# A three-stage kernel for one NeuronCore: three of the run-up rounds of its recurrence made before the last attention block is finished

## The chip, the cores and the metric

The kernel runs on one core of a Trainium2 chip, in one launch. The metric is the device time of that launch in microseconds (us). All data is float32.

## The reference, cut to what matters

The input x has 4 batches of 128 channels and 64 by 64 = 4096 tokens. Three layers follow each other:

- Layer 0 is attention over all tokens with 64 channels per head row, and its output is added to x.
- Layer 1 is causal attention with 128 channels over the normalised tokens, and its output is added too.
- The last layer normalises the tokens, multiplies them by W, normalises each of the 128 channels over all batches and tokens (a batch norm: mean and variance of 4 x 4096 values), and runs a recurrence along the tokens. Its result is added to the tokens:

```
Wx = (flat - mean) * rsqrt(var + eps) * gamma + beta
y[t] = sigmoid(Wx[t] + y[t-1] @ V.T)        # y[-1] = 0, 4096 tokens, 4 batches
```

The 4096 steps of the recurrence depend on each other. V is orthogonal and the slope of the sigmoid is at most 0.25, so a wrong start is forgotten within some rounds.

## The kernel before, in words

`fast_path` does the work. A second path, `general_path`, follows in the program and is entered only if a flag says that a result is out of range.

**Attention.** The tokens of a batch are 8 blocks of 512. A long list of items (a block of queries against a pair of key tiles) is worked off in one loop: `scores` puts a product into the PSUM tile `s_ps` (two buffers of two banks each, pool `ps_s`) and an exponential on ACT (L937), `values` two items later multiplies the exponentials `p` into `acc` (L990), and `sums` adds them up on DVE (L961, L969). What a finished block still needs hangs on chains of steps with due times (`finish0`, `finish1`), which the loop takes up between items.

**The last block** (batch 3, block 7) has a short form of its own in `finish1`, marked `final`. PE sums the softmax denominators (`den_ps`, L615); ACT and DVE each copy half of `acc` into `agg` (L1010, L1011); four products with `wv1` (`o_ps`, L643) are added to the tokens on DVE (L667); DVE takes moments (L676, L677), POOL raises to the power -0.5 (L681), and DVE and ACT each scale two of four tiles into `xh` (L695, L693). PE transposes them (`xh2T_ps`, L821), DVE and ACT each copy half (L822), PE multiplies by W (`wx_ps`, L851), DVE takes statistics of it (`ends`, L852) and ACT copies it into the tensor `xs` (L853). PE has two groups of idle work there, `warm_ps` (L790): 9 products after `o_ps` and 6 after `wx_ps`, whose results nobody reads. `spare` (L796) is a sigmoid of one column, which loads the sigmoid's table into ACT.

**Statistics.** Each block's `wx_ps` gives statistics into `stats`. When 31 of the 32 blocks are done, `ahead` (L730 to L732) folds them into three numbers of `ends`; the last block adds two more groups, and after it `mv` (L1171) and eight small instructions (L1175 to L1183) make `scale`, `shift` and `shift_half`, the batch norm as one multiplication and one addition.

**The recurrence.** The 4096 tokens of a batch are cut into 256 chunks of 16 steps, and all chunks of a batch run side by side as 256 columns. One round is one step of all chunks of the four batches: for each batch a product with V on PE (`y_ps`, L1222), a multiplication and addition on DVE (`z`, L1224) and a sigmoid on ACT (L1228). A chunk's start is not known, so ten run-up rounds (`WARM = 10`, steps -10 to -1) go over the last ten steps of the chunk before. The first of them starts from an assumed state of 0.5 and needs no product: it is one sigmoid per batch on ACT (L1219). Round -1 writes `start`. Rounds 0 to 15 give the result.

From round 4 on, each round has a `residual` after batch 1: four transposes on PE and one addition on DVE to `xr` (L1260), which is then sent out (L1261). POOL makes the sums of batches 0 and 1 from `xc` (`add`, L1235), sent out by L1237; the tile `sum` has three buffers. Both `xc` (8 loads of 512 KB, L1158) and `xr` (4 loads of 1 MB, L1168) are copies of the tokens that wait in DRAM, in `x2c` and `x2t`; all loads and outputs are issued by SP, in order. At the end `meet` (L1244 to L1248) squares the gap between each chunk's end and the start that the next chunk assumed, sums the squares per channel, and `judge` sets the flag.

**What orders the work.** Each engine has one queue and works it off in order. The order is made by a scheduler, except where `keep_in_program_order` pins an instruction. Waits between engines are counts on semaphores. A pool that is opened where older pools lay in memory makes its tiles wait for the last users of that memory: `xc`, `xr`, `mv` and `start` lie where the pools of the attention lay.

Of the kernel before, what the change touches and what calls it, by code (L numbers as in the profile page):

```python
# [9 lines left out]
F32 = mybir.dt.float32  # L10
# [350 lines left out]
def fast_path(  # L361
# [31 lines left out]
    WARM, TOL = 10, 2e-6  # L393
# [17 lines left out]

    def load(engine, name, shape, *parts):
        t = const.tile(shape, F32, name=name)
        for dst, src in parts:
            engine.dma_start(out=dst(t), in_=src)
        return t
# [22 lines left out]
    fold = const.tile([P, P], F32, name="fold")  # L439
# [22 lines left out]
    g1 = const.tile([P, P], F32, name="g1")  # L462
# [8 lines left out]
    spare = const.tile([P, 1], F32, name="spare")  # L471
# [10 lines left out]
    with tc.tile_pool(name="batch", bufs=1) as batch, tc.tile_pool(name="rows", bufs=2) as rowp, tc.tile_pool(  # L482
# [120 lines left out]
        def folded(den, by_pe):  # L603


            sq = wk.tile([P, TPB, Q, S], F32, tag="sq", name="sq")
            nc.vector.transpose(out=sq.rearrange("p j q s -> p (j q s)"), in_=den)
            part = stat.tile([P, Q, TPB], F32, tag="part", name="part")
            nc.vector.tensor_reduce(part, sq.rearrange("p j q s -> p q j s"), AX.X, ALU.add)
            own = stat.tile([P, Q, TPB], F32, tag="own", name="own")  # L610
            if by_pe:


                dp = misc("den_ps")[:, : TPB * Q]
                nc.tensor.matmul(dp, lhsT=fold, rhs=part.rearrange("p q j -> p (q j)"), start=True, stop=True)  # L615
                ins = nc.vector.tensor_tensor(own, dp.rearrange("p (q j) -> p q j", q=Q), quarter, ALU.mult)
                if copied:

                    tc.add_manual_dep(
                        ins.ins,  # L620
                        copied[0].ins.name,
                        mybir.DependencyInfo(mybir.DependencyClass.NoSync, mybir.DependencyReason.DATA),
                        reason="order on DVE",
                    )
            else:

                by_token = dram2.tile([Q, S, Q, TPB], F32, tag="by_token", name="by_token")
                for k in range(Q):
                    nc.sync.dma_start(out=by_token[:, :, k].rearrange("q r j -> r q j"), in_=part[ts(k, S)])
                nc.sync.dma_start(out=own, in_=by_token.rearrange("q r k j -> (q r) k j"))  # L630
            return own
# [7 lines left out]
        def projected1(agg):  # L639

            op = misc("o_ps")
            for j in range(TPB):
                nc.tensor.matmul(op[:, ts(j, P)], lhsT=agg[:, ts(j, P)], rhs=wv1, start=True, stop=True)  # L643
            return op
# [41 lines left out]
        def normed(b, g, dst, mv, half, y, last=False):  # L686

            newton(y, half, stat.tile([P, TPB], F32, tag="z", name="ln_z"), not last)
            for j in range(TPB):
                if last:  # L690
                    t = xs[:, b, ds(g * BLK + j * P, P)]
                    if j % 2:
                        nc.scalar.activation(dst[:, j], t, AF.Copy, scale=y[:, j : j + 1])  # L693
                    else:
                        nc.vector.tensor_scalar(dst[:, j], t, y[:, j : j + 1], None, ALU.mult)  # L695
                    continue
                nc.vector.tensor_scalar(  # L697
                    dst[:, j], xs[:, b, ds(g * BLK + j * P, P)], mv[:, j, 0:1], y[:, j : j + 1], ALU.subtract, ALU.mult
                )
# [27 lines left out]
        def ahead():  # L727

            mv = stat.tile([P, nc.vector.BN_AGGR_DIM], F32, tag="mv1", name="mv1")
            nc.vector.bn_aggr(mv, stats)  # L730
            nc.vector.tensor_copy(ends[:, 1:2], mv[:, 0:1])
            nc.vector.tensor_tensor(ends[:, 2:3], mv[:, 1:2], ends[:, 0:1], ALU.mult)  # L732

# [46 lines left out]
        def finish1(b, g, turn):  # L780
# [4 lines left out]
            def warm(n, rhs):  # L785

                ps = ps_s.tile([P, 2 * BLK], F32, tag="s", name="warm_ps")
                for _ in range(n):
                    tc.keep_in_program_order(
                        nc.tensor.matmul(ps[:, : BLK // 2], lhsT=ident, rhs=rhs, start=True, stop=True)  # L790
                    )

            def first():
                if final:

                    nc.scalar.activation(spare, agg[:, 0:1], AF.Sigmoid)  # L796
                denominators(1, b, g, mem["own"])
                joined(1, b, g, mem["op"] if turn else projected1(agg))
                if final:
                    warm(9, agg[:, : BLK // 2])  # L800
# [13 lines left out]
            def second():  # L814
                mem["xhT"] = wk.tile([P, BLK], F32, tag="xhT2", name="xhT2")
                if final:
                    for k, copy in enumerate((nc.vector.tensor_copy, nc.scalar.copy)):
                        ps = misc("xh2T_ps")
                        for i in range(2):

                            nc.tensor.transpose(ps[:, ts(i, P)], mem["xh"][:, 2 * k + i], ident)  # L821
                        copy(mem["xhT"][:, ts(k, BLK // 2)], ps[:, : BLK // 2])  # L822
                    return
# [21 lines left out]
            def third():  # L845

                to = xs[:, b, ts(g, BLK)].rearrange("p (s c) -> p s c", s=STEPS)
                if final:
                    for k in range(2):
                        wp = misc("wx_ps")[:, : BLK // 2]  # L850
                        nc.tensor.matmul(wp, lhsT=wfc, rhs=mem["xhT"][:, ts(k, BLK // 2)], start=True, stop=True)  # L851
                        nc.vector.bn_stats(ends[:, 3 + 6 * k : 9 + 6 * k], wp)  # L852
                        nc.scalar.copy(to[:, :, ts(k, CPB // 2)], wp.rearrange("p (c s) -> p s c", s=STEPS))  # L853
                    warm(6, mem["xhT"][:, : BLK // 2])
                    return
# [13 lines left out]
            def sums():  # L869
                mem["own"] = folded(den, by_pe)  # L870
# [41 lines left out]
        def scores(it):  # L912
# [16 lines left out]
            else:  # L929
# [7 lines left out]
                nc.scalar.activation(it.p[:, :off], ps[:, :off], AF.Exp, scale=float(P) ** -0.5)  # L937
# [33 lines left out]
        def values(it):  # L971
# [16 lines left out]
            else:  # L988
                for h, (t, q0, n, o) in enumerate(it.at):
                    nc.tensor.matmul(  # L990
# [5 lines left out]
                    )  # L996
            if it.last:
# [9 lines left out]
                else:  # L1007
                    bt.agg = wk.tile([P, BLK], F32, tag="agg", name="agg")
                    if it.b == B - 1 and it.g == NB - 1:
                        nc.scalar.copy(bt.agg[:, : BLK // 2], bt.acc[:, 0, : BLK // 2])  # L1010
# [64 lines left out]
        def begin(s):  # L1075
            nonlocal done
            if done < s < len(items):
                done = s
                it = items[s]
                if it.first:  # L1080
# [4 lines left out]
                scores(it)  # L1085

# [62 lines left out]
    with tc.tile_pool(name="xr", bufs=1) as xrp, tc.tile_pool(name="y", bufs=2) as yp, tc.tile_pool(  # L1149
# [22 lines left out]
        one = lambda name: xrp.tile([P, 1], F32, name=name)  # L1172
        var, y, half, nmean, z = one("var"), one("y0"), one("var_half"), one("nmean"), one("z0")
        scale, shift, shift_half = one("scale"), one("shift"), one("shift_half")
        nc.vector.tensor_scalar(var, mv[:, 1:2], BN_EPS, None, ALU.add)  # L1175
        nc.gpsimd.tensor_tensor(y, var, mhalf[:, :1], ALU.pow)
        nc.vector.tensor_scalar(half, var, -0.5, None, ALU.mult)
        nc.vector.tensor_scalar(nmean, mv[:, 0:1], -1.0, None, ALU.mult)
        nc.vector.scalar_tensor_tensor(z, in0=y, scalar=half, in1=y, op0=ALU.mult, op1=ALU.mult)
        nc.vector.scalar_tensor_tensor(y, in0=z, scalar=1.5, in1=y, op0=ALU.add, op1=ALU.mult)  # L1180
        nc.vector.tensor_tensor(scale, y, gamma, ALU.mult)
        nc.vector.scalar_tensor_tensor(shift_half, in0=nmean, scalar=scale, in1=beta_half, op0=ALU.mult, op1=ALU.add)
        nc.vector.scalar_tensor_tensor(shift, in0=nmean, scalar=scale, in1=beta, op0=ALU.mult, op1=ALU.add)  # L1183

        by_step = xs.rearrange("p b (g s c) -> p b s g c", s=STEPS, c=CPB)
        start = xrp.tile([P, B, NCH + 1], F32, name="start")
        nc.gpsimd.memset(start[:, :, 0:1], 0.0)
        prev = [None] * B
        grid = lambda t: t.rearrange("p (g c) -> p g c", c=CPB)
# [14 lines left out]
        pin = tc.keep_in_program_order  # L1204

        def step(b, s):
# [11 lines left out]
            if prev[b] is None:  # L1218
                nc.scalar.activation(grid(y), wx, AF.Sigmoid, scale=scale, bias=shift_half)  # L1219
            else:  # L1220
                ps = ps_y.tile([P, NCH], F32, tag=f"y{b}", name="y_ps")
                order(nc.tensor.matmul(ps if s < 1 else shaped(ps), lhsT=vf, rhs=prev[b], start=True, stop=True))  # L1222
                z = yp.tile([P, NCH], F32, tag=f"z{b}", name="z")
                ins = nc.vector.scalar_tensor_tensor(  # L1224
                    grid(z), in0=wx, scalar=scale, in1=grid(ps), op0=ALU.mult, op1=ALU.add
                )
                order(ins)
                order(nc.scalar.activation(y, shaped(z), AF.Sigmoid, bias=shift))  # L1228
# [13 lines left out]
        def meet(b):  # L1242
# [5 lines left out]
            nc.scalar.activation(sq, ps, AF.Square, accum_out=gap[:, b : b + 1])  # L1248
# [37 lines left out]
        def judge():  # L1286
            total = xrp.tile([P, 1], F32, name="total")
            tc.keep_in_program_order(nc.vector.tensor_scalar(count[:, :B], gap, TOL * TOL, None, ALU.is_le))
# [70 lines left out]
```

## Time and profile before

| What | us |
|---|---|
| median of 3 runs (2024.64 to 2025.42) | 2025.14 |
| the profiled execution's own time | 2024.73 |
| its span in the profile | 2023.0 |
| last exponential of the attention starts | 1946.7 |
| first sigmoid of the recurrence starts | 1961.6 |
| round -1 starts on ACT | 1978.15 |
| the flag is written | 2019.56 |

The profile is one execution, taken by the hardware profiler; its times are counted from the start of the span, and 1.7 us of the execution lie around it. PE is busy for 99% of the span, DVE for 72%, ACT for 48% and POOL for 7%. A row "start, us, engine, line, operation, out<-in, xN" is one group of instructions; brackets at its end give the engine's idle time before it and what ended that. PEld is the weight load of a product. A float32 product is two passes on PE, so a line's count of records is twice its products.

### The profile page before, as it was taken

How to read it: one execution, taken by the hardware profiler on the slowest of the kernel's cores; microseconds unless marked ns; L12 is line 12 of the kernel's file. 1: busy time of each engine (PE TensorE's matmuls, PEld its weight loads, DVE VectorE, ACT ScalarE, POOL GpSimd, SP SyncE). 2: the span in 40 equal slices, each digit the busy share in tenths (PEclk: the TensorE clock that was granted, in tenths of full speed). 3: DMA queues.
4: the chain of work that ended last, by engine and by line, in shares of the span. 5: the costliest groups of instructions: out<-in, count | busy, mean ns of one | idle time of the engine just before them, and what ended most of it. 6: DMA issues, size and time to landing. Idle time of an engine off the chain costs nothing.

```text
span 2023.0 us, 31281 instructions
## 1 busy us (share of the span) xinstructions
PE 2011.7 (99%) x11902; PEld 878.1 (43%) x11902; DVE 1460.2 (72%) x2814; ACT 975.9 (48%) x1055; POOL 139.8 (7%) x237
## 2 busy tenths in 40 slices
PE   9999999999999999999999999999999999999998
PEld 3333354444333345444433334444433333544457
DVE  4799877555789987555589997655478998765568
ACT  5666633332666653333466663333356665333347
POOL 1000011000000001000000001000000000100004
PEclk9999999999999999999999999999999999999999
DMA  3111112220210112330111111231010111120046
GB/s 105 44 33 23 22 33 57 61 47 16 43 52 15 23 23 40 71 68 16 43 47 35 22 23 33 48 83 33 16 43 2 23 23 23 37 48 22 16 96 254
DMA packets 238443, 89.02 MB, mean 44 GB/s; under 512 B 174816, under 2 KB 219360, under 8 KB 237776
## 3 DMA queue, kind: packets, MB, share of 16 engines
q1 hardware_dynamic: 237280, 86.42, 18.0%
q8 instruction: 94, 1.54, 0.3%
q14 instruction: 61, 0.50, 0.1%
q0 software_dynamic: 288, 0.39, 0.1%
q10 hardware_dynamic: 720, 0.16, 0.0%
HBM read 45.84 MB, written 36.89 MB: 41 GB/s over the span
## 4 chain that ended last, share of the span: by engine, by line
PE 96%; DVE 2%; ACT 2%; issue 0%; DMA 0%; POOL 0%; POOLq 0%; ACTq 0%
PE s_ps L934 23%; PE acc L990 22%; PE s_ps L921 22%; PE acc L981 22%; PE o_ps L643 1%; PE r_ps L596 1%; PE wx_ps L857 1%; PE kr_ps L534 1%; DVE z L1224 1%; PE v_ps L546 1%; PE o_ps L653 1%; ACT y L1228 1%; DVE xr L1260 0%; ACT xs L1228 0%; PE warm_ps L496 0%
## 5 line engine op out<-in xcount | busy, mean ns | idle before, releaser
L961 DVE TENSOR_TENSOR dsum<-dsum,p 128x1024 f32<-128x1024 f32 x692 | 845.5, 1222 | 403.8 <-ACT p L937 296.1
L928 ACT ACTIVATE p<-s_ps,nshift 128x1024 f32<-128x1024 f32 x512 | 570.1, 1117 | 312.4 <-PE s_ps L921 296.8
L937 ACT ACTIVATE p<-s_ps 128x1024 f32<-128x1024 f32 (+2 forms) x288 | 274.2, 952 | 601.8 <-PE s_ps L934 580.0
L981 PE MATMUL acc<-p,v 64*64 64x512 f32 x4096 | 530.2, 589 | 0.0
L921 PE MATMUL s_ps<-kr,swap 64*64 64x512 f32 x2048 | 524.7, 590 | 1.5 <-ACT p L928 1.3
L921 PE MATMUL s_ps<-kr 64*64 64x512 f32 x2048 | 522.4, 590 | 0.0
L934 PE MATMUL s_ps<-rows,xhT 128*128 128x512 f32 (+3 forms) x1152 | 500.7, 558 | 0.0
L990 PE MATMUL acc<-p,xh 128*128 128x512 f32 (+3 forms) x1152 | 500.2, 557 | 0.0
L934 PEld LDWEIGHTS s_ps<-rows,xhT 128*128 128x128 f32 x1152 | 215.0, 190 | 244.7 <-issue 202.9
L990 PEld LDWEIGHTS acc<-p,xh 128*128 128x128 f32 x1152 | 216.2, 190 | 239.7 <-issue 223.3
L981 PEld LDWEIGHTS acc<-p,v 64*64 64x64 f32 x4096 | 157.1, 133 | 283.0 <-issue 274.7
L921 PEld LDWEIGHTS s_ps<-kr,swap 64*64 64x64 f32 x2048 | 141.9, 133 | 145.8 <-issue 135.8
L921 PEld LDWEIGHTS s_ps<-kr 64*64 64x64 f32 x2048 | 141.6, 133 | 135.5 <-issue 134.0
L681 POOL TENSOR_TENSOR ln_rstd<-ln_var,mhalf 128x4 f32<-128x4 f32 x64 | 69.9, 1092 | 1185.7 <-DVE ln_var L679 1185.7
L969 DVE TENSOR_TENSOR dsum<-dsum,p 128x256 f32<-128x256 f32 (+1 forms) x120 | 56.1, 501 | 60.9 <-POOL p L941 60.9
L667 DVE SCALAR_TENSOR_TENSOR xs<-o_ps,recs,xs 128x128 f32<-128x128 f32 x256 | 70.5, 344 | 5.1 <-PE o_ps L653 1.7
L697 DVE TENSOR_SCALAR xh<-xs,ln_mv,ln_rstd 128x128 f32<-128x128 f32 x252 | 70.2, 342 | 1.9
L676 DVE BATCH_NORM_STATS2 ln_st<-xs 128x6 f32<-128x128 f32 x256 | 62.9, 272 | 0.0
L941 POOL TENSOR_SCALAR_AFFINE_SELECT p<-p 128x128 f32<-128x128 f32 x128 | 34.5, 294 | 374.4 <-ACT p L937 368.8
L959 DVE COPY dsum<-p 128x1024 f32<-128x1024 f32 x44 | 30.2, 687 | 25.0 <-ACT p L937 15.2
L711 DVE STREAM_TRANSPOSE sqT<-xh 128x512 f32<-128x512 f32 x63 | 44.7, 709 | 1.7
L1224 DVE SCALAR_TENSOR_TENSOR z<-xs,scale,y_ps 128x256 f32<-128x256 f32 x100 | 43.4, 478 | 1.9 <-PE y_ps L1222 1.6
(149 smaller groups left out, 877.1 us busy)
## 6 DMA issues: line engine op xcount, KB each, us to landing
xs<-in_xT SPq DMA_DIRECT2D x32, 256.0 KB, 3.1
by_r<-sqT SPq DMA_DIRECT2D x128, 64.0 KB, 2.2
xhT<-by_r SPq DMA_DIRECT2D x128, 64.0 KB, 2.0
by_c<-sqT SPq DMA_DIRECT2D x124, 64.0 KB, 1.8
xhT<-by_c SPq DMA_DIRECT2D x31, 256.0 KB, 2.8
xs<-in_x SPq DMA_DIRECT2D x12, 512.0 KB, 5.5
swap<-kr SPq DMA_DIRECT2D x32, 128.0 KB, 2.3
x2c<-sqT SPq DMA_DIRECT2D x64, 64.0 KB, 2.3
```

The costliest lines, as they stand in the source:

```text
L667: nc.vector.scalar_tensor_tensor(t, in0=op[:, ts(j, P)], scalar=rec[:, j : j + 1], in1=t, op0=ALU.mult, op1=ALU.add)
L676: nc.vector.bn_stats(st[:, j], xs[:, b, ds(g * BLK + j * P, P)])
L681: nc.gpsimd.tensor_tensor(y, var, mhalf, ALU.pow)
L697: nc.vector.tensor_scalar(dst[:, j], xs[:, b, ds(g * BLK + j * P, P)], mv[:, j, 0:1], y[:, j : j + 1], ALU.subtract, ALU.mult)
L921: nc.tensor.matmul(ps[c * M : c * M + M, ts(r, BLK)], lhsT=keys[:, ts(c, M)], rhs=rows[r], start=True, stop=True,)
L928: nc.scalar.activation(it.p, ps, AF.Exp, bias=nshift)
L934: nc.tensor.matmul(ps[:, off : off + n], lhsT=lhsT, rhs=rhs, start=True, stop=True)
L937: nc.scalar.activation(it.p[:, :off], ps[:, :off], AF.Exp, scale=float(P) ** -0.5)
L961: nc.vector.tensor_tensor(flat, flat, it.p, ALU.add)
L981: nc.tensor.matmul(bt.acc[c * M : c * M + M, r], lhsT=bt.v[part, m * TPB + j, h], rhs=it.p[part, ts(c, BLK)], start=it.first, stop=it.last,)
L990: nc.tensor.matmul(bt.acc[:, 0, q0:], lhsT=bt.xh[:, t], rhs=it.p[:, o : o + n], start=it.first and h == 0, stop=it.last and h == 1,)
L1224: ins = nc.vector.scalar_tensor_tensor(grid(z), in0=wx, scalar=scale, in1=grid(ps), op0=ALU.mult, op1=ALU.add)
```

## The change

The diff, cut to what the prediction speaks of:

```diff
-    WARM, TOL = 10, 2e-6
+    AHEAD, WARM, TOL = 3, 6, 2e-6
...
+    joint = const.tile([P, 2 * B, P], F32, name="joint")
+    slots = iter(range(2 * B))
     def load(engine, name, shape, *parts):
-        t = const.tile(shape, F32, name=name)
+        t = joint[:, next(slots)] if shape == [P, P] else const.tile(shape, F32, name=name)
...
+    near = const.tile([P, P], F32, name="near")
+    warmed = joint.rearrange("p k c -> p (k c)").rearrange("p (b c) -> p b c", b=B)
+    def affine(mv, pool, name):
...
+        return scale, shift, shift_half
...
         def ahead():
...
+            most.extend(affine(mv, const, "most"))
+            nc.vector.tensor_scalar(near, ident, most[0], None, ALU.mult)
+        most, early = [], []
+        WHOLE = [(b, 0, NB) for b in range(B - 1)] + [(B - 1, 0, NB - 1)]
+        LAST = (B - 1, NB - 1, NB)
+        def early_states(i, b):
+            return warmed[:, b] if i == AHEAD - 1 else early[0][:, i, ts(b, NCH)]
+        def early_place(i, b, g0, g1):
+            if not early:
+                states = batch.tile([P, 2, N // 2], F32, tag="kr", name="early")
+                early.extend([states] + [ps_s.tile([P, 2 * BLK], F32, tag="s", name="early_ps") for _ in range(2)])
...
+        def early_input(i, b, g0, g1):
+            _, at, wx = early_place(i, b, g0, g1)
+            pin(nc.tensor.matmul(grid(at), lhsT=near, rhs=wx, start=True, stop=False))
+        def early_product(i, b, g0, g1):
+            cols, at, _ = early_place(i, b, g0, g1)
+            pin(nc.tensor.matmul(at, lhsT=vf, rhs=early_states(i - 1, b)[:, cols], start=False, stop=True))
+        def early_sigmoid(i, b, g0, g1):
...
+            if i:
+                pin(nc.scalar.activation(y, at, AF.Sigmoid, bias=shift))
+            else:
+                pin(nc.scalar.activation(grid(y), wx, AF.Sigmoid, scale=scale, bias=shift_half))
+        def early_step(i, part):
+            early_input(i, *part)
+            early_product(i, *part)
+            early_sigmoid(i, *part)
...
             def first():
-                if final:
-                    nc.scalar.activation(spare, agg[:, 0:1], AF.Sigmoid)
...
                 if final:
-                    warm(9, agg[:, : BLK // 2])
+                    early_product(1, *WHOLE[0])
+                    early_sigmoid(1, *WHOLE[0])
+                    for part in WHOLE[1:]:
+                        early_step(1, part)
+                    early_step(2, WHOLE[0])
...
             def second():
                 if final:
+                    early_step(2, WHOLE[1])
...
+                    early_input(2, *WHOLE[2])
                     return
...
             def third():
...
-                    warm(6, mem["xhT"][:, : BLK // 2])
+                    early_product(2, *WHOLE[2])
+                    early_input(2, *WHOLE[3])
+                    early_product(2, *WHOLE[3])
+                    early_input(1, *LAST)
+                    early_input(2, *LAST)
+                    early_sigmoid(0, *LAST)
+                    for i in range(1, AHEAD):
+                        early_sigmoid(2, *WHOLE[1 + i])
+                        early_product(i, *LAST)
+                        early_sigmoid(i, *LAST)
                     return
...
             def sums():
-                mem["own"] = folded(den, by_pe)
+                mem["own"] = folded(den, by_pe, final)
+                if final:
+                    early_input(1, *WHOLE[0])
...
                 scores(it)
+                if last:
+                    for part in WHOLE:
+                        early_sigmoid(0, *part)
...
-        prev = [None] * B
+        prev = [warmed[:, b] for b in range(B)]
...
-            nc.scalar.activation(sq, ps, AF.Square, accum_out=gap[:, b : b + 1])
+            nc.scalar.activation(sq, ps, AF.Square)
+            nc.scalar.activation(sq, sq, AF.Square, accum_out=gap[:, b : b + 1])
...
-            tc.keep_in_program_order(nc.vector.tensor_scalar(count[:, :B], gap, TOL * TOL, None, ALU.is_le))
+            tc.keep_in_program_order(nc.vector.tensor_scalar(count[:, :B], gap, TOL**4, None, ALU.is_le))
```

In words: `affine` holds the eight small instructions that make scale and shift; `ahead` now calls it too, with the statistics of 31 blocks (`most`), and makes `near`, a diagonal matrix of that scale. Three rounds, called 0, 1 and 2 here, are made with it. In the code W0 to W3 are the four batches (W3 without the last block, 224 columns instead of 256), and LAST is the last block's 32 columns. Round 0 is a sigmoid on ACT straight from `xs`. In rounds 1 and 2 PE makes the input itself, `near` times the columns of `xs`, and adds the product with V in PSUM; ACT takes the sigmoid from there, and DVE has no part. Both PSUM tiles `early_ps` take the place of the two `s_ps` buffers: batches 0 and 1 share one tile, 2 and 3 the other. The states of rounds 0 and 1 lie in a tile `early` of the attention's pool (the place of `kr`), those of round 2 in the place of eight weight matrices, now one tile `joint`. `spare` and both groups of `warm_ps` are gone. Several instructions of the last block are now pinned on PE and ACT. Six run-up rounds (steps -6 to -1) follow in place of ten, all with a product. `meet` squares twice, and the limit is the fourth power of the same tolerance.

## The prediction

> **What bounds the kernel now.** I read the page's chain of waits first. In order of time, from the last block on, it says (start us, duration us, what):
>
> ```profile
> 1950.57 0.40 PE den_ps L615 x2
> 1950.97 1.16 PE o_ps L643 x8
> ...
> 1956.76 0.42 PE xh2T_ps L821 x2
> ...
> 1957.68 1.13 PE wx_ps L851 x4
> 1958.81 2.60 PE warm_ps L790 x12
> ...
> 1961.57 2.08 ACT y L1219 x4
> 1963.64 14.51 ACT y L1228 x32
> 1978.15 1.81 ACT start L1228 x4
> ```
>
> The last block holds the end for 11 us (1950.5 to 1961.5), through all engines in turn. Then ten run-up rounds follow, bound by ACT: eight take 14.51, so 1.81 each. (The `warm_ps` line stands in for the statistics on DVE, which end at 1961.38.) From round 4 DVE is the bound, at 2.17 a round, and its queue holds additions to `xr`:
>
> ```profile
> 1987.56 0.69 DVE L1260 TENSOR_TENSOR xr<-xr,yT_ps 128x512 f32<-128x512 f32 x1
> 1988.17 1.65 DVE L1224 SCALAR_TENSOR_TENSOR z<-xs,scale,y_ps 128x256 f32<-128x256 f32 x4
> ...
> 1994.07 0.68 DVE L1260 TENSOR_TENSOR xr<-xr,yT_ps 128x512 f32<-128x512 f32 x1
> ```
>
> Those additions need the loads of `xr`. So the next views are SP's timeline, the page's row of issues (its last column: median us from issue to landing), and a table of windows (last columns: DMA share, GB/s):
>
> ```profile
> 1950.55 0.30 SPq L1158 DMA_DIRECT2D xc<-x2c  x1
> 1953.31 0.38 SPq L802 DMA_DIRECT2D x2t<-xs  x1
> 1953.74 4.26 SPq L1158 DMA_DIRECT2D xc<-x2c  x7
> 1958.05 7.08 SPq L1168 DMA_DIRECT2D xr<-x2t  x4
> ```
> ```profile
> xr<-x2t SPq DMA_DIRECT2D x4, 1024.0 KB, 21.2
> ```
> ```profile
> 1957.00:1973.00 16.00, 14.90 (x67) 10.29 (x66) 12.68 (x34) 12.56 (x29) 0.55 (x1) 1.00 1.06 210
> ...
> 1978.00:1981.00 3.00, 3.00 (x14) 1.95 (x13) 2.96 (x8) 3.00 (x8) 0.03 (x1) 1.00 1.00 412
> ```
>
> The DMA engines are full from 1953 to 1984. Eight loads of `xc` run at 210 GB/s and the landings show 2.56 us each, the last at 1975.0; then four of `xr` at 412 GB/s, landing from 1977.4 to 1986.0. The fourth addition to `xr` starts at 1994.07, so today 8.1 us are spare. Nothing on the chain shows these loads, and they are hidden only because the first was issued at 1950.55.
>
> **What the change removes.** Four rounds of 1.81: but the first old round had no product, and the new first one has, behind a `z` of 0.48. Old: the first sigmoid at 1961.57, round -1 at 1978.15. New: `z` right behind `shift` (0.02), the first sigmoid 0.51 after it, five rounds of 1.82 to round -1, so 9.63 after `shift` against 16.77 (1961.38 to 1978.15). That is **-7.1** if `shift` stays where it is.
>
> **What it adds before the last block's end.** Prices: a pass of 256 columns 0.216 on PE, its result 0.38 after the last one's start; a product that had to wait takes 0.10 more (the first `y_ps` takes 0.74 to its `z`, others 0.63); ACT to PE 0.05, PE to ACT 0.09. A sigmoid of 256 columns from PSUM is not in the trace: the square from PSUM takes 0.383, the copy 0.372, the sigmoid from SBUF 0.508; I take 0.383, the same source on the same engine, and keep 0.51 as upper end (+0.6 over five in a row).
>
> Free, as far as I see: the nine DVE instructions of the early statistics take 1.81 (the old group L1175 to L1183) and 0.28 for `near` (as `xh`), from 1941.3 to 1943.4. DVE idles 0.85 there, the next `dsum` then ends at 1944.6, and DVE waits for POOL until 1945.70 anyway. Without that cover it would cost up to 2.1. The table load (1.28) and four sigmoids (0.495 apart, as L1219) fit on ACT between the last exponential (ends 1947.19) and the end of `acc` (1950.48): 1950.46.
>
> Not free: PE and ACT now hand over to each other. In the list of waits of the changed program, the input of W1 waits for the sigmoid of W0 of the same round, and W3 for W2: they write other columns, but the same PSUM tile. In queue order:
>
> - PE: the first input (0.43) stands before `o_ps`, which ends 0.2 later. Product, then sigmoid(1,W0) to 1953.2.
> - Only then input and product of W1 (4 passes), and W2 behind them: sigmoid(1,W2) to 1955.8. Only then W3: sigmoid(1,W3) to 1957.3; sigmoid(2,W0) to 1958.2.
> - ACT's half of `xh` (1956.32 before) stands behind these sigmoids: 1958.2 to 1958.9. On PE, input and product of (2,W1) stand before the transposes and wait for sigmoid(2,W0): 1958.25 to 1959.2. So the transposes start at 1959.2, before 1956.75: **+2.5**.
> - The same work then follows with an input (0.43) between, hidden under the copy of `xhT`: statistics of `wx_ps` to 1961.7, copies into `xs` to 1962.1 (1959.69 before).
> - The inputs of LAST wait for that copy: 1962.9. Sigmoid(2,W2) counts on them: 1963.35. Product(1,LAST) 1963.8, sigmoid 1964.1, sigmoid(2,W3) 1964.4, product(2,LAST) **1964.9**. The short products are priced as `den_ps` (0.40), the short sigmoids as `spare` (0.20).
>
> **The added wait.** `mv` in the changed program waits for that last product, since `early` lies in the old pools' memory. It starts at 1964.95, before 1959.32: +5.6. DVE has nothing else queued; everything after needs it. So `shift` comes at 1967.0, round -1 at 1976.65: only **1.5 earlier** than before.
>
> The first load of `xc` waits for the same product: its place in memory is that of `early`. Behind it on SP stand seven more loads and the four of `xr`. Issue at 1964.97, 14.4 later than now. By the old rows: first landing after 4.8, seven more 2.56 apart, then 10.9 from the last `xc` (1975.04) to the last `xr` (1985.95): 33.6. One of the sixteen shares of that last load landed 1.15 behind the others; without that, 32.5. So the last `xr` lands at **1998.6**.
>
> The fourth addition would be due at 1994.07 - 1.5 = 1992.6. It waits 6 us (the first already 4: due at 1986.1, its load lands at 1990.0), and DVE is the bound from there, so nothing is caught up. Against before: 1998.65 - 1994.07 = **+4.6**.
>
> **The end.** `meet` has a second square per batch; the last one is on the chain: 0.383 and a wait, 0.40 to 0.50, I take **+0.45**. The other three lie under PE.
>
> **The sum.** +4.6 + 0.45 = +5.0, on the profiled execution's own 2024.73: **2029.7**, with the median of the runs shown (2025.14) 0.4 above that execution. Lower end of the unknown terms: no late share (-1.15), cheaper hand-overs (-1); upper end: sigmoids at 0.51 and all hand-overs at 0.1 more (+1.3). The case alone: 2027.5 to 2031.
>
> [...] The granted clock reads 1.00 in every window of the trace, with the idle products in place. [...]
>
> **The rivals.**
>
> *The loads are not the bound.* If the last `xr` lands before 1992.6, only the rounds and the end count: -1.5 + 0.45 = -1.0, **2023.7**: not slower. It decides when the loads start by 1959.0 (1992.6 - 33.6). For it: before, they start at 1950.55, and -1.0 is what the rounds are worth by my walk. Against: the wait list, and a DMA share of 1.00 to 1.06 which leaves no faster loads. A chance of 0.17, with what lies between it and the forecast.
>
> *The gaps hold everything.* ACT and PE have gaps in the last block (ACT idles 3.33 and 3.92 us), PE fills the places of 15 products that cost nothing, and `mv` and the loads come some 5 us earlier than I walk: -7.1 + 0.45 = -6.6, **2018.1**. Against: 14 more products, and hand-overs of about 1.5 us each in a queue that was never idle that long. 0.05.
>
> *POOL and the outputs end last.* `add` can start only when all of `xc` is there (1987.8), and its outputs queue behind `xr` until 1998.6; three buffers of `sum` are full by then. From there 13 additions of 1.54 end at 2019.2 and the last outputs land near 2022, under the flag, which by my sum comes at 2024.6. It decides from the point where an output takes over 3.1 us to land (two additions; the page has 2.2 to 2.3, with a DMA share of 0.65 to 0.74, and here the outputs come at POOL's pace, so about 0.68 x 2.17 / 1.54 = 0.96). At 4.4 us, twice the page's, an addition comes every 2.0 us, the last outputs land at 2028, and the end is some 3 later than the forecast: 2033. 0.13.
>
> *The flag is set*, and the general path runs: thousands of us, no row prices it. Run over the reference's own inputs, the recurrence with 3 and 6 rounds gives a largest fourth root of 1.1e-6, against a limit of 2e-6. 0.02.
>
> **How the numbers follow.** The forecast has 0.63. Of it about 0.22 lies within 0.2% (4 us, about what a measurement of this kernel can tell from no change), since its lower end is at +2.8; 0.41 above. With POOL (0.13) and the general path (0.02) slower has 0.56. Within: 0.22 and 0.17, 0.39. Faster: 0.05. The range goes down to 2025.0, which leaves out the third case and most of the second, and up to 2033.0.
>
> **What the profile of after would show.** The first `xc` issued near 1965; DVE idle before `xr` 4, then about 0.3 to 0.5 three times, released by the loads; `mv` at 1965; transposes of the last block at 1959; round -1 near 1976.7; ACT rows of the early rounds that wait for PE and PE rows that wait for ACT in turn. I am wrong if `xc` is issued before 1960, if DVE does not wait before `xr`, or if the walk is off by over 2 us.

## The result, and the profile after

| | before | after |
|---|---|---|
| median of 9 runs each | 2024.97 us | 2030.79 us |
| lowest and highest | 2024.64, 2025.73 | 2030.04, 2032.41 |
| the profiled execution's own time | 2024.73 us | 2032.41 us |

The ratio is 1.0029, with an interval of 1.0019 to 1.0039: the change costs 5.8 us. The forecast was 2029.7. One thing has to be known before the profile is read: its execution is the highest of the nine, 1.6 above their median.

SP's timeline of the changed kernel (start, duration, what) has the loads where the walk had put them, at 1964.97 and 0.4 more, since this execution reached the last exponential 0.4 later (1947.11 in place of 1946.70):

```profile
1965.54 4.40 SPq L1247 DMA_DIRECT2D xc<-x2c  x8
1970.69 8.02 SPq L1257 DMA_DIRECT2D xr<-x2t  x4
```

DVE's timeline (in brackets the idle time before, and what ended it) shows `mv` held by the last early product, and then the four additions to `xr`:

```profile
1965.50 0.22 DVE L1260 BATCH_NORM_AGGREGATE mv<-ends 128x2 f32<-128x15 f32 x1 [3.23 <-PE early_ps L792]
...
1992.18 0.69 DVE L1331 TENSOR_TENSOR xr<-xr,yT_ps 128x512 f32<-128x512 f32 x1 [5.15 <-DMA xr<-x2t]
...
1994.67 0.69 DVE L1331 TENSOR_TENSOR xr<-xr,yT_ps 128x512 f32<-128x512 f32 x1 [0.23 <-DMA xr<-x2t]
...
1998.53 0.69 DVE L1331 TENSOR_TENSOR xr<-xr,yT_ps 128x512 f32<-128x512 f32 x1 [0.37 <-PE yT_ps L1326]
...
2001.24 0.69 DVE L1331 TENSOR_TENSOR xr<-xr,yT_ps 128x512 f32<-128x512 f32 x1
```

The first two wait for their loads, as forecast. The third waits for PE, and that was in no step of the forecast. The table of windows gives the reason (columns: window, its length, busy time of PE, PEld, DVE, ACT and POOL, granted clock, DMA share, GB/s):

```profile
1990.00:1992.00 2.00, 0.00 (x0) 0.00 (x0) 0.00 (x0) 0.00 (x0) 1.93 (x2) 1.00 1.00 414
1992.00:1994.00 2.00, 0.14 (x1) 0.15 (x1) 1.82 (x5) 0.70 (x2) 2.00 (x2) 0.66 1.03 426
1994.00:1996.00 2.00, 2.00 (x5) 1.64 (x6) 1.55 (x5) 1.22 (x4) 0.55 (x1) 0.50 0.99 410
1996.00:1998.00 2.00, 2.00 (x7) 1.53 (x7) 1.25 (x3) 1.31 (x3) 0.00 (x0) 0.50 0.99 405
1998.00:2000.00 2.00, 2.00 (x9) 1.72 (x8) 1.39 (x4) 0.61 (x2) 0.00 (x0) 0.63 1.00 352
2000.00:2002.00 2.00, 2.00 (x13) 1.77 (x12) 2.00 (x5) 1.78 (x4) 1.56 (x2) 1.00 0.07 25
```

While DVE waits, PE has nothing to do; then its clock is halved for 6.8 us, and `y_ps` holds the chain. The same table has an earlier loss, just before the rounds:

```profile
1963.00:1965.00 2.00, 0.78 (x6) 0.55 (x5) 0.00 (x0) 1.23 (x4) 0.00 (x0) 1.00 0.00 0
1965.00:1967.00 2.00, 1.56 (x5) 1.28 (x6) 0.96 (x7) 0.29 (x2) 0.66 (x2) 0.58 0.22 35
1967.00:1969.00 2.00, 2.00 (x7) 1.62 (x6) 1.57 (x6) 0.84 (x2) 0.00 (x0) 0.56 0.80 197
```

### The profile page after: what moved, and what is told of

Its sections match the earlier page's. It is cut to its first block, busy times and chain, and to the rows that moved or that the text cites. A ratio compares the mean times of both kernels' runs of the same rounds, so it can differ in the third digit from the quotient of the medians.

```text
span 2030.6 us, 31253 instructions
## 1 busy us (share of the span) xinstructions
PE 2012.2 (99%) x11888; PEld 879.3 (43%) x11888; DVE 1456.6 (72%) x2811; ACT 977.0 (48%) x1057; POOL 140.1 (7%) x238
## 4 chain that ended last, share of the span: by engine, by line
PE 96%; DMA 2%; DVE 1%; ACT 0%; issue 0%; POOL 0%; POOLq 0%; ACTq 0%; DVEq 0%
PE s_ps L1015 22%; PE acc L1073 22%; PE s_ps L1002 22%; PE acc L1064 22%; PE o_ps L671 1%; PE r_ps L622 1%; PE wx_ps L936 1%; PE kr_ps L560 1%; DMA xr<-x2t 1%; PE v_ps L572 1%; PE o_ps L683 1%; DVE z L1294 1%; PE y_ps L1292 0%; DMA xc<-x2c 0%; DVE xr L1331 0%; PE early_ps L787 0%
## 5 line engine op out<-in xcount | busy, mean ns | idle before, releaser
L941 ACT COPY xs<-wx_ps 128x512 f32<-128x512 f32 x31 | 18.1, 585 | 50.4 <-DVE stats L937 48.3
```

## The experiments

**Theory:** the loads, held until the last early product, make the additions to `xr` late, and that is the loss. **Rivals:** the hand-overs in the last block; the clock; POOL and the outputs; the second square.

The table has every kernel that ran. "Moved" is its median less that of the kernel before on the same chip. The four columns on the right are times in the one profiled execution, counted from the start of the last exponential, so that the early part's jitter (up to 1.3) is out of them: round -1 on ACT, first and fourth addition to `xr`, flag.

| kernel | median | moved | round -1 | 1st add | 4th add | flag |
|---|---|---|---|---|---|---|
| before | 2024.97 | | 31.38 | 40.86 | 47.36 | 72.85 |
| after | 2030.79 | +5.8 | 30.39 | 45.07 | 54.13 | 80.01 |
| early states among the constants | 2024.88 | -0.3 | 30.79 | 40.29 | 46.79 | 72.68 |
| before, loads held | 2031.12 | +5.9 | 31.39 | 45.03 | 53.03 | 78.52 |
| after, 24 idle products | 2037.60 | +12.4 | 30.68 | 44.80 | 57.04 | 82.93 |
| constants, other order | 2022.19 | -3.0 | 26.14 | 35.64 | 42.15 | 68.03 |
| the same, PE kept busy | 2020.20 | -5.0 | 26.12 | 35.62 | 42.13 | 68.01 |
| after, PE kept busy | 2030.82 | +5.6 | 30.12 | 45.22 | 53.48 | 79.36 |
| after, 11 idle products | 2030.54 | +5.3 | 30.74 | 45.05 | 52.56 | 78.38 |
| constants, PE kept busy | 2023.45 | -1.8 | 29.21 | 38.71 | 45.21 | 71.10 |
| before, nine rounds | 2023.94 | -1.1 | 29.56 | 39.05 | 45.56 | 71.44 |
| after, other order | 2028.01 | +3.0 | 27.61 | 41.92 | 49.89 | 75.77 |
| after, loads swapped | 2046.43 | +21.4 | 30.82 | 40.32 | 46.82 | 72.86 |
| before, no idle products | 2028.15 | +3.1 | 34.77 | 44.27 | 50.77 | 76.27 |

### The hold taken away

```diff
+    firsts = const.tile([P, B * NCH], F32, name="firsts")
...
-            return warmed[:, b] if i == AHEAD - 1 else early[0][:, i, ts(b, NCH)]
+            return warmed[:, b] if i == AHEAD - 1 else firsts[:, ts(b, NCH)]
...
-                states = batch.tile([P, 2, N // 2], F32, tag="kr", name="early")
...
```

Round 1 overwrites round 0 here. To make room, `vT` shares its buffers with `sqv`, far ahead of the last block.

> The changed kernel, but the states of the early rounds lie in a tile of the constants, so that no load and no instruction of the statistics waits for the last early product; all the rest stays. Theory (the held loads, and what the wait for them does, carry the loss): the first load of xc is issued near 1951 as before the change, DVE does not wait before any addition to xr, the clock of PE stays at 1.00. The last early product still ends near 1965.1 and PE has its first product of the rounds behind it, so the first z comes at about 1966.1 (1967.59 with the change) and round -1 near 1976.1, 2.5 earlier than before the change (1978.15, and 0.4 for the later start of this execution); with 0.45 for the second square: 2.0 under the kernel before, 2023.0, and 7.8 under the changed one. Rival (the hand-overs in the last block and the second square carry it): the time stays within 1 us of the changed kernel's 2030.8.

Measured: 2024.88. The loads are issued early again, and no addition waits (40.29, and 6.50 on to the fourth). SP and DVE of this kernel:

```profile
1950.77 0.30 SPq L1247 DMA_DIRECT2D xc<-x2c  x1
```
```profile
1987.20 0.69 DVE L1331 TENSOR_TENSOR xr<-xr,yT_ps 128x512 f32<-128x512 f32 x1
...
1993.71 0.68 DVE L1331 TENSOR_TENSOR xr<-xr,yT_ps 128x512 f32<-128x512 f32 x1
```

So the held loads are worth some 6 (+5.8 against -0.3), and the theory stands. The edit frees `mv` as well (it starts at 1962.24 in place of 1965.50), but round -1 is no earlier for it (30.79 against 30.39), so the gain is that of the loads. The forecast of 2023.0 is missed by 1.9. This kernel's PE timeline and windows show where:

```profile
1963.86 0.41 PE L792 MATMUL early_ps<-firsts,vf 128*128 128x32 f32 x2 [0.56 <-ACT joint L800]
1964.99 0.41 PE L792 MATMUL early_ps<-firsts,vf 128*128 128x32 f32 x2 [0.72 <-ACT joint L800]
1965.78 3.64 PE L1292 MATMUL y_ps<-joint,vf 128*128 128x256 f32 x8 [0.38 <-ACT joint L800]
```
```profile
1964.00:1966.00 2.00, 0.90 (x5) 0.68 (x6) 0.30 (x2) 0.91 (x3) 0.00 (x0) 0.99 1.05 213
1966.00:1968.00 2.00, 2.00 (x6) 1.54 (x6) 0.73 (x2) 0.51 (x1) 0.00 (x0) 0.50 1.05 198
```

The eight passes of the first round take 3.64: the clock is at 0.50. (In the kernel with the other order, profiled at 1.00, the same row takes 1.99.) PE never waited longer than 0.72, but since 1962.8 it had only had passes of 32 columns.

### The hold alone

The kernel before, with the twelve loads, in their order, behind the second run-up round:

```diff
+        def loads(late):
+            nc.gpsimd.tensor_copy(xc[:, :, 0, 0], late[:, 0:BY_C])
...               (the twelve dma_start of xc and xr, pinned)
                 step(b, s)
+                if (s, b) == (1 - WARM, 2):
+                    loads(prev[b])
```

> The kernel before, with all its rounds and products, but the twelve loads wait for a small POOL copy of the second run-up round's result, so that the first is issued near 1965.3, as in the changed kernel. Theory: DVE waits about 4 us before the first addition to xr (its load lands near 1991.8), PE is idle for over 4 us and runs at half its clock for some 5 to 7 us behind, the fourth addition starts 6 to 7 later than the 1994.07 of before, and the whole takes 2030.5 to 2031.5. If the clock does not drop, the loads alone give the last landing at 1999 and +4.9: 2029.9. Rival (the loss is in the last block and the end): within 0.5 of the kernel before, 2025.0.

Measured: 2031.12, so +5.9 without a single early round, hand-over or second square. SP and DVE of this kernel:

```profile
1965.96 4.82 SPq L1164 DMA_DIRECT2D xc<-x2c  x8
```
```profile
1992.45 0.69 DVE L1262 TENSOR_TENSOR xr<-xr,yT_ps 128x512 f32<-128x512 f32 x1 [4.11 <-DMA xr<-x2t]
```

The late loads, with the loss of clock behind their stall (0.50 from 1996 to 1998 here, too), suffice for the whole.

### What the clock adds behind the stall

Two runs of the changed kernel with products without use, behind the transposes of the second group (`n` is 24 and then 11):

```diff
+            if (s0, b, h) == (0, BY_C, 1):
+                idle_ps = ps_r.tile([P, TPB, P], F32, tag="r", name="idle_ps")
+                for _ in range(n):
+                    pin(nc.tensor.matmul(idle_ps[:, :2], lhsT=ident, rhs=start[:, 0, 1:], start=True, stop=True))
             part = ds(s0, TPB)
```

> The changed kernel, and behind the transposes of the second addition's group 24 products without use (0.22 us each, 5.2 in all), which fill most of PE's idle time while DVE waits for xr. Theory (one load is late, and then the clock): the first addition still starts near 1992.2 behind the same wait, but the clock stays at 1.00, the fourth addition starts at about 1998.7 to 1999.1 in place of 2001.24, and the time falls by 2 to 2.5, to 2028.5. Rival (each of the four loads is late by itself): the fourth addition and the time stay as they are, 2030.8 within 0.5, with DVE idle for a DMA before each. If the products stand in the way instead: above 2031.

Measured: 2037.60, a miss of my own making. A float32 product is two passes; the 24 took 10.36 in the chain (`idle_ps`, x48) and stood in the way.

> The changed kernel, with 11 products without use behind the transposes of the second addition's group, 4.75 in all: the run before with 24 had counted one pass for each, where each has two. Theory (four late loads and, on top, the loss of clock behind the stall): the clock stays at 1.00 from 1990 on, the additions start as their loads land, at 1992.2, 1994.7, 1997.2 and 1999.7, so the fourth comes 1.5 earlier than 2001.24, and the time is 2029.3 (2028.8 to 2029.8). Rival (the loads alone set the four additions, the clock is hidden behind them): 2030.8 within 0.4. If only the first load were late, and the clock did the rest: 2028.5 or less.

Measured: 2030.54. In its profile the additions fall where the loads land, one by one:

```profile
1992.22 0.69 DVE L1335 TENSOR_TENSOR xr<-xr,yT_ps 128x512 f32<-128x512 f32 x1 [4.75 <-DMA xr<-x2t]
...
1994.72 0.69 DVE L1335 TENSOR_TENSOR xr<-xr,yT_ps 128x512 f32<-128x512 f32 x1 [0.25 <-DMA xr<-x2t]
...
1997.21 0.69 DVE L1335 TENSOR_TENSOR xr<-xr,yT_ps 128x512 f32<-128x512 f32 x1 [0.24 <-DMA xr<-x2t]
...
1999.74 0.69 DVE L1335 TENSOR_TENSOR xr<-xr,yT_ps 128x512 f32<-128x512 f32 x1 [0.27 <-DMA xr<-x2t]
```

So in this one execution the fourth is 1.5 earlier than in the profile of the change, as the theory said, but the medians differ by 0.25, as its rival said. Both hold: the changed kernel's executions spread over 2.4 (2030.0 to 2032.4), these over 0.5 (2030.2 to 2030.7). By this spread I estimate that the loss of clock costs between nothing and 2, by execution, and little in the median. The mean clocks agree: in the changed kernel with PE kept busy before the rounds (next section), the three executions at 2032.0 and above have one of 0.998 and the six up to 2031.5 one of 0.999. Read from the one profile alone, it would have been put at 1.5.

### What the clock costs before the rounds

Three products without use: one before each of the last two early products (with the other order: both before the second), one behind. `unused(n)` issues `n` products of 256 columns into a PSUM tile that nobody reads.

```diff
                     for i in range(1, AHEAD):
                         early_sigmoid(2, *WHOLE[1 + i])
+                        unused(1)
                         early_product(i, *LAST)
                         early_sigmoid(i, *LAST)
+                    unused(1)
```

> The changed kernel, with three products without use in the same places (one ahead of each of the last two early products, one behind). Theory: the first loss of clock (0.5 to 0.67 from 1965 to 1968.6) goes and round -1 comes some 1.5 earlier, but the first addition to xr waits for its load until 1992.1 as before, PE is idle that much longer, and the time stays within 0.5 of 2030.8. Rival (the first loss of clock is part of the 5.8): some 1.5 to 2 less, 2029.

Measured: 2030.82, the time of the changed kernel. Its clock is at 1.00 from 1960 to 1971, and nothing comes of it, since the first addition waits for its load in any case (5.57, against 5.15).

> The kernel with the states among the constants (2024.9, clock 0.5 from 1966 to 1969.2), with one product without use ahead of each of the last two early products and one behind. Theory (the loss of clock in the first round is what that run missed of its forecast): clock 1.00, the first round's eight passes take 1.75 in place of 3.65, and the time is 2023.0, within 0.5. Rival (the walk of that run was wrong elsewhere): 2024.9 within 0.4.

Measured: 2023.45, 1.4 less than without them; by the flag of the profiles 1.6. The miss of the first run is explained by the clock, but for some 0.4.

### The hand-overs

One line more, on the kernel with the states among the constants (in the last of these runs on the changed kernel itself):

```diff
         LAST = (B - 1, NB - 1, NB)
+        WHOLE[1:3] = WHOLE[2:0:-1]
```

> As the run with the early states among the constants, and besides batch 2 goes before batch 1 in the early rounds, so that PE's input of the next batch writes the PSUM tile that ACT does not read at that time. Theory (hand-overs through the shared tile cost about 0.8 each, two of them ahead of the transposes): the sigmoids of the second early round come 0.86 apart, the transposes of the last block at about 1958.4 in place of 1959.8, the last early product near 1963.7, and the time 1.4 under the run with the constants alone, 2021.6. Rival (the waits are covered by the statistics of the block, which end the last block anyway): the same time as that run, within 0.4.

Measured: median 2022.19, on two levels: 4 of 11 executions at 2019.4 to 2019.9, 7 at 2022.1 to 2022.4. In the profiled one the transposes start at 1956.70, which is 10.35 after the last exponential (12.67 in the changed kernel), and no row of PE shows a wait for ACT ahead of them any more. So the hand-overs were worth 2.3 there, not the 1.4 that I gave them.

> The kernel with the states among the constants and batch 2 ahead of batch 1, and besides three products without use on PE (0.43 each): two while it waits for the last sigmoids ahead of the last early product, one behind it. That kernel has two levels: 4 of 11 executions at 2019.4 to 2019.9, with a mean clock of 1.000, and 7 at 2022.1 to 2022.4, with 0.999. Theory (PE's sparse stretch before the rounds, in which it waits at most 0.7 at a time, lets the clock fall in some executions for the first round): all executions at 2019.4 to 2020.0, clock 1.000. Rival (the two levels come from elsewhere, from the loads or the early part): both levels stay; or the products stand in the way: above 2022.

Measured: nine executions from 2019.7 to 2020.6, one level, median 2020.20: 0.9976 of the kernel before (0.9966 to 0.9986). The 0.6 to the level of 2019.6 is not the products: counted from the last exponential both profiles have the same times within 0.02. This is the fastest kernel of the study, 5.0 under the one before. With PE kept busy in both orders (2023.45 and 2020.20), the order is worth 3.2.

> The changed kernel with its early states where they were, and only the order of the batches in the early rounds changed (batch 2 ahead of batch 1). Theory (the loads wait for the last early product, and the end moves with them one to one): that product ends at 1961.7 as in the run with both edits, in place of 1965.5, the first load is issued at 1961.8, and everything behind moves by 3.75: 2026.8, within 0.6, with DVE still waiting for the first addition's load. Rival (the hand-overs are covered by something else): 2030.5 to 2030.8.

Measured: 2028.01, less gain than expected. SP and DVE of this kernel:

```profile
1962.58 4.44 SPq L1248 DMA_DIRECT2D xc<-x2c  x8
```
```profile
1989.11 0.69 DVE L1332 TENSOR_TENSOR xr<-xr,yT_ps 128x512 f32<-128x512 f32 x1 [4.78 <-DMA xr<-x2t]
```

The first load is 3.0 earlier than in the changed kernel, not 3.75; the first addition is 3.1 earlier, the median 2.8. The end does move with the loads nearly one to one; I had taken the start of the loads from a kernel whose execution ran 0.8 earlier.

### One part alone: fewer rounds

```diff
-    WARM, TOL = 10, 2e-6
+    WARM, TOL = 9, 2e-6
...
-            nc.scalar.activation(sq, ps, AF.Square, accum_out=gap[:, b : b + 1])
+            nc.scalar.activation(sq, ps, AF.Square)
+            nc.scalar.activation(sq, sq, AF.Square, accum_out=gap[:, b : b + 1])
```

(The limit becomes `TOL**4` as well.)

> The kernel before with one part of the change alone: the limit on the fourth power (a second square for each batch) and nine run-up rounds in place of ten, none of them early, which is as many as the change makes in all. Theory (a round is worth 1.81 while the loads have room, the square costs 0.4 to 0.45 at the end): 1.4 less, 2023.8. If the loads or POOL bind already: 2025.2 to 2025.6, no gain.

Measured: 2023.94. By the profile round -1 comes 1.82 earlier and the flag 1.41, so the squares cost 0.4.

### One part alone: no idle products

```diff
-                    warm(9, agg[:, : BLK // 2])
+                    pass
...
-                    warm(6, mem["xhT"][:, : BLK // 2])
```

> The kernel before without the 15 products that have no use (nine behind the projection of the last block, six behind its last product), the one part of the change that was costed at nothing as long as PE waits no longer than about 1 us at a time. Theory (a sparse stretch on PE lowers its clock whatever the single waits are): PE has little to do between 1952 and 1962, the clock falls to 0.5 when the rounds begin, the eight passes of a round take 3.4 in place of 1.75 for one to two rounds, and the time is 2026.7 to 2028.3. Rival (the products cost and bring nothing): 2025.1 within 0.4. If the clock falls in some executions only: two levels, 2025 and 2027.

Measured: 2028.15, +3.1. PE's timeline and two windows of this kernel:

```profile
1956.81 1.09 PE L821 MATMUL xh2T_ps<-ident,xh 128*128 128x128 f32 x4 [4.64 <-DVE xh L695]
1957.99 2.08 PE L851 MATMUL wx_ps<-xhT,wfc 128*128 128x256 f32 x4
1963.32 7.07 PE L1221 MATMUL y_ps<-y,vf 128*128 128x256 f32 x19 [3.25 <-ACT y L1218]
```
```profile
1958.00:1960.00 2.00, 2.00 (x4) 1.17 (x4) 0.43 (x1) 0.55 (x2) 0.00 (x0) 0.50 1.06 214
...
1966.00:1968.00 2.00, 2.00 (x6) 1.60 (x5) 0.97 (x3) 1.31 (x3) 0.00 (x0) 0.50 1.06 197
```

Two idle stretches, 4.64 and 3.25, and the clock is at half from 1956 until 1968. `wx_ps` takes 2.08 in place of 1.13, and PE bounds the first rounds (5.48 of `y_ps` in the chain). The products that nobody reads are worth 3.1.

### The loads in the other order

The four loads of `xr` are issued ahead of the eight of `xc`, all pinned.

> The changed kernel with the four loads of xr issued ahead of the eight of xc. Theory: xr lands from 1970 to 1979, DVE never waits for it, the clock keeps to 1.00 behind round 4, and the flag comes near 2019.5, 7.5 earlier; but xc is there only at 1999, POOL's sixteen additions of 1.54 then end at 2024 and their last output lands near 2026.5, so POOL and the outputs end the kernel: 2028 to 2030. Rival (POOL's work is not near the end): 2023.3. Rival (the order of the loads does not matter, their start does): 2030.5 to 2030.8.

Measured: 2046.43; all expectations missed. The first half came true: no addition waits, and the flag comes as early as before the change (72.86). But SP's queue was ordered otherwise, too, as its timeline shows; below it is the first row on outputs in the list of waits (total, times, longest):

```profile
1967.74 11.82 SPq L1253 DMA_DIRECT2D xc<-x2c  x8
2014.25 0.95 SPq L1331 DMA_DIRECT2D out_x<-xr  x2
2015.30 4.66 SPq L1306 DMA_DIRECT2D out_x<-sum  x4
```
```profile
POOL sum L1304 <- DMA out_x<-sum: 15.4, 2, 14.0
```

Two outputs of `xr` that go out only at 2014 stand ahead of the first output of `sum`; POOL, with three buffers, stands still for 14.0. What POOL costs with outputs in a good order stays open.

## Why the prediction was right, and where its size was off

In the order of its steps, in times from the last exponential, forecast against the profile of the change:

- **Early statistics and first sigmoids free:** right. They end at 1943.65 and 1950.96, and the chain does not see them.
- **Hand-overs, +2.5 for the transposes:** 1959.78 against 1956.76, less 0.4 for the late start: +2.6. PE waits 0.56 for ACT three times before them, as walked:

```profile
1953.80 0.70 PE L787 MATMUL early_ps<-xs,near 128*128 128x256 f32 x2 [0.56 <-ACT early L800]
...
1956.36 0.65 PE L787 MATMUL early_ps<-xs,near 128*128 128x224 f32 x2 [0.56 <-ACT early L800]
...
1958.81 0.70 PE L787 MATMUL early_ps<-xs,near 128*128 128x256 f32 x2 [0.56 <-ACT joint L800]
```

  A sigmoid of 256 columns from PSUM took 0.47, between the 0.383 that I took and the 0.51 that I kept as upper end.
- **The added wait, `mv` and first load:** 18.25 and 18.27 forecast, 18.39 and 18.43 measured.
- **Round -1, 1.5 earlier:** 1.0 earlier; with the clock kept, 1.3.
- **Fourth addition, +4.6:** the mis-sized step. It came 6.8 later in the profiled execution, the highest of nine. Where the clock is kept (11 idle products) it came 5.2 later: in the profile of the change the loads took 34.1 from the first issue to the last landing (33.6 forecast), and the last early product was 0.15 later. The rest is the clock: DVE waited for the first two loads (5.15 before the first, 4 forecast), but before the third for PE.
- **Second square, +0.45:** 0.39 (from the fourth addition to the flag: 25.88 against 25.49).
- **No term for the clock:** wrong, twice. I had costed the 15 products at nothing as long as PE waits no longer than about 1 at a time, which no row of before shows; the clock fell all the same, from 1.00 to 0.50, with waits of 0.72 at most. And I had looked for idle time before the rounds only: the stall that I forecast myself makes PE idle for 4.7, and 6.8 at a clock of 0.50 follow. That it hardly matters for the median was luck: the late loads cover the first loss wholly and most of the second.
- **15 idle products cost nothing to take away:** next to nothing in this kernel, for the same reason (three in their place bring no gain: 2030.82 against 2030.79). In the kernel before, where the loads are not late, the 15 are worth 3.1; three are worth 1.4 and 2.0 where the states lie among the constants.

Of the rivals, *the loads are not the bound* gave 2023.7 for early loads, and its condition was not met. With early loads and the clock kept, 2023.45 was measured, which is near its price, but not for its reasons: in that kernel `mv` does not wait either, round -1 comes 2.2 earlier and not 1.5, and the median is 1.8 under the kernel before, not 1.0. *The gaps hold everything* (2018.1) is what the kernel with the other order, early loads and a busy PE comes near to, at 2020.20. *POOL and the outputs* did not end the kernel: POOL's last addition ended at 2021.55, and the flag came at 2027.12. POOL did stand still once for 5.9 behind its first three additions, as this rival had it: the first output was issued at 1991.62 and landed at 2000.29, POOL went on at 2000.44. (The profile of the change puts this wait down to ACT, that of the kernel with 11 idle products, 5.8 there, to the output.) It had the time to spare.

## What to carry to other kernels

Before work is moved into a gap, look whose memory its results take: here a tile of 16 KB per partition in an old pool held twelve loads that nothing on the chain had shown, and moving it to its own place turned +5.8 into -0.3, with the order of batches and a busy PE into -5.0. A buffer shared by two engines in turn made them wait for each other here even on different columns (the two halves of one PSUM tile; PE waited 0.56 three times); alternating the buffers took these waits away and brought the transposes 2.3 earlier. And compare the profiled execution with the median before a number is taken from it.

## What the runs showed of the hardware

- **The granted clock fell without a long wait.** In the kernel with the early states among the constants, 3.0 us with eight passes of 32 columns and waits of 0.38 to 0.72 were followed by a clock of 0.50 from 1966 to about 1969.4; with three more products of two passes each (twelve such passes took 2.60 before, so 0.43 a product) in the same place it stayed at 1.00. With the other order the thin stretch is 2.3 us long, and the clock fell in 7 of 11 executions (by their mean clock, 0.999 against 1.000), for 2.6 us of time.
- **The stretches at half the clock were 3.4 us long here, or a multiple of it.** From the windows (length times twice what the clock lacks to 1.00): 3.4 before the rounds of the changed kernel (2 x 0.84 + 2 x 0.88), 6.8 behind its stall (2 x 0.68 + 4 x 1.00 + 2 x 0.74), 3.4 behind the stall of the kernel before with its loads held (2 x 0.68 + 2 x 1.00 + 2 x 0.04), and 13.6 in the kernel without idle products. So much the same stall cost 3.4 there and 6.8 here.
- In the profiles of before and after the change, most of the eight loads of 512 KB landed 2.4 to 2.7 apart at about 200 GB/s, and most of the four of 1 MB 2.3 to 2.5 apart at about 410; one load in each came some 1 us later than that (before, the second of `xr`, 3.6 behind the first; after, the seventh of `xc`, 3.9 behind the sixth). From the first issue to the last landing the twelve took 35.4 before and 34.1 after.
